# Two-layer network on one core: layer 1's expert places from running sums made batch by batch, with the expert stage begun earlier and its broadcasts spread out

## The chip, the cores and the metric

The kernel runs on one core of one Trainium2 chip. The number that counts is the device time of one execution in microseconds, as the median of several runs. Five engines work side by side, each through its own queue in order: TensorE (PE, with weight loads shown apart as PEld), VectorE (DVE), ScalarE (ACT), GpSimd (POOL) and SyncE (SP), which here only issues transfers.

## What is computed

Two layers over 16 sequences of 512 tokens with 128 features (8192 tokens). Layer 0 adds to its input a memory that is trained chunk by chunk and a transformer block with a dense mixture of 8 experts. Layer 1 adds causal attention (16 heads, a convolution, then a second attention pass over the same keys and values) and a routed mixture of 32 experts, of which each token chooses 8:

```python
x = L0_attn_x
xn = _layernorm(x, axis=-1)
x = x + _L0_attn_ref(xn, ...) + _L0_ffn_ref(xn, ...)
xn = _layernorm(x, axis=-1)
x = x + _L1_attn_ref(xn, ...) + _L1_ffn_ref(xn, ...)
```

The part that matters is the routing in `_L1_ffn_ref`. An expert takes at most 128 tokens, the first 128 in token order that chose it:

```python
probs = jax.nn.softmax(logits.astype(jnp.float32), axis=-1)
topw, topi = jax.lax.top_k(probs, TOP_K)
...
oh = jax.nn.one_hot(flat_e, E, dtype=jnp.int32)
pos = (jnp.cumsum(oh, axis=0) * oh).sum(-1) - 1
buf = jnp.zeros((E, CAPACITY, H), x.dtype).at[flat_e, pos].set(flat_x, mode='drop')
```

So for place c of expert e the kernel must find which token has it: the token at which the running count of choices of e reaches c + 1.

## The kernel before

**Turns.** All work is written as Python generators ("stages"). `Turns.run` steps every live stage once a turn, in the order of a small number given to each stage: 0 for `tops` (scores and their maxima, `largest`), 1 for `back` (scores again, exponentials, weighted values, `weighted`), 2 for `summed`, 3 for the expert stage `moe`, 4 for the projections and `middle`, 5 for `total`. PE's queue is exactly in this order, written out by hand. The queues of DVE, ACT, POOL and SP are put in order by the framework's scheduler, which goes by the program's order and by its own picture of when an instruction's inputs are ready. At the end of a turn with little PE work, `fill` adds a matmul of no use (L206).

Eleven turns make one unit of attention: for a quarter of a batch's work, row blocks of 512 (four turns), 384 (four), 256 (two) and 128 columns (one). In each turn two PSUM banks of scores go to DVE for the maxima (L396 for the wide ones, L403 and L404 for the narrow) and two to ACT for the exponentials (L476); POOL, and after the mark `counted` DVE (L482), clears what lies above the diagonal. Seven PSUM banks go round. `room` and `hold` limit how many of them the other stages may keep beyond a turn (`pools["work"]`: 3, then 2).

**Routing.** `middle(b)` ends layer 0 for batch b and routes it. It writes for each tile of 128 tokens the running counts by expert to the table `ctab` in DRAM (L1246) and each tile's totals into one column of `totT`, 32 experts by 64 tiles, in SBUF (L1247), eight transfers a batch on SP's queue; then it stores tokens and weights (`xw`, L1254) and marks `("xw", b)`.

**The expert stage.** `moe` starts when all batches are routed. Its first part sums `totT` along the tiles with six steps of two DVE instructions (L1349, L1350: shifts by 1, 2, 4, 8, 16, 32). `places(u)`, for eight experts at a time, multiplies the sums by a mask (`bd`, L1358), has PE broadcast them to 128 partitions (`pt`, two matmuls), counts on DVE how many tiles lie before each place (`le`, `istar`, L1366 and L1367) and takes the largest sum among them (`base`, L1369 and L1371). `side` starts the four `places` one turn apart. From these come the row indices `rowi` (L1376). POOL then gathers 32 rows of `ctab` (`gt`, L1387), DVE counts within each (`lt`, L1381), and the token indices follow. After that come 16 pairs of experts, one begun every third turn: POOL gathers the tokens (`xg`, L1425), PE and ACT compute, DVE weighs the result (`eo`, L1464), and POOL adds it to `acc` in DRAM by a scatter (L1470). Each scatter waits for the one before. When `moe` is marked, `total` copies the batches whose attention was added early straight to the output (L1497, thirteen of them) and adds up the others (L1500 to L1505).

**Around the change.** Layer 0's buffers `fa` are closed when its attention is done, and `fb` opens in their place; the exponentials then alternate between buffers in `att` and `mid`, later between `att` and `fb`. `lent` holds the exponentials in `mid` that are not used yet. The end of `network` reads, in the kernel before:

```python
turns.run(until=lambda: ("xw", B - 1) in done)
pools.update(weights=[att, fb])
turns.run(until=lambda: not lent)
...
pools["work"] = 2
turns.stages.append((turns.turn, 3, moe(mo)))
```

The second `run` waits until the last exponentials in `mid` have been read; only then is `mid` closed, `mo` opened in its place and `moe` begun. At the same time batch 15's projections for attention run (`front1`): `split_rows` writes `hi` (ACT, L333) and `lo` (DVE, L335), one buffer each, and stores each with two transfers (L339), first for the queries, two turns later for the keys.

Of the kernel before, what the change touches and what calls it, by code (L numbers as in the profile page):

```python
# [9 lines left out]
F32 = mybir.dt.float32  # L10
# [7 lines left out]
P = 128  # L18
# [64 lines left out]
def network(ctx: ExitStack, tc: tile.TileContext, a, out):  # L83
# [189 lines left out]
    def idle(n):  # L273
        for _ in range(n):
            yield
# [920 lines left out]
    def middle(mid, b):  # L1196

        yield from after(("ffn", b))
        ac = mid.tile([P, TB, D], F32, tag="am", bufs=2, name="am")
        nc.sync.dma_start(flat(ac), x1d[0, b])  # L1200
        xa = mid.tile([P, TB, D], F32, tag="st", bufs=4, name="xa")
        nc.sync.dma_start(xa, acc_b[b])
        x2 = mid.tile([P, TB, D], F32, tag="st", bufs=4, name="x2")
        yield from idle(2)
        yield from layernorm(x2, ac, row["g2"], row["b2n"])
        nc.gpsimd.tensor_tensor(x2, x2, xa, ALU.add)
        yield from idle(3)
# [12 lines left out]
        yield from room()  # L1220
        prl = work("prl")[:, 0 : TB * EXP1].rearrange("p (t e) -> p t e", e=EXP1)
        for t in range(TB):
            mm(prl[:, t, :], xT[:, t * P : (t + 1) * P], D1("gw"))
        lg = sm.tile([P, TB, EXP1], F32, tag="lg", name="lg")
        nc.scalar.copy(lg, prl)
        yield
        t8 = sm.tile([P, TB, TOPK], F32, tag="t8", name="t8")
        lr = sm.tile([P, TB, EXP1], F32, tag="lr", name="lr")
        for t in range(TB):
            nc.vector.max(t8[:, t, :], lg[:, t, :])  # L1230
            nc.vector.match_replace(lr[:, t, :], t8[:, t, :], lg[:, t, :], -BIG)
# [12 lines left out]
        for t in range(TB):  # L1244
            of = ct[EXP1 * t : EXP1 * (t + 1), :]
            nc.sync.dma_start(ctab_v[:, b * TB + t, :], of)  # L1246
            nc.sync.dma_start(totT[:, b * TB + t : b * TB + t + 1], of[:, P - 1 : P])  # L1247
        yield
        nc.vector.tensor_tensor(lg, lg, lr, ALU.mult)
        sw = sm.tile([P, TB], F32, tag="sw", name="sw")  # L1250
        nc.vector.tensor_reduce(sw, lg, AX.X, ALU.add)
        nc.vector.reciprocal(sw, sw)
        nc.vector.tensor_tensor(xwt[:, :, D:], lg, bc(sw, 2, EXP1), ALU.mult)
        nc.sync.dma_start(xw_b[b], xwt)  # L1254
        mark("xw", b)
        yield


# [79 lines left out]
    rowi = mw.tile([P, EXP1], I32, name="rowi")  # L1338
    tok = mw.tile([P, EXP1], F32, name="tok")

    def moe(mo):

        memE = load(mo, "mske", [EXP1, EXP1])

        cur = totT
        s_ = 1
        while s_ < NTILE:
            nxt = mo.tile([EXP1, NTILE], F32, tag=f"cum{s_}", bufs=1, name=f"cum{s_}")
            nc.vector.tensor_copy(nxt[:, 0:s_], cur[:, 0:s_])  # L1349
            nc.vector.tensor_tensor(nxt[:, s_:], cur[:, s_:], cur[:, : NTILE - s_], ALU.add)  # L1350
            cur, s_ = nxt, 2 * s_
        per = 512 // NTILE

        def places(u):

            es = slice(u * per, (u + 1) * per)
            bd = ff.tile([EXP1, per, NTILE], F32, tag="ew1", bufs=2, name="bd")
            nc.vector.tensor_tensor(bd, bc(cur, 1, per), bc(memE[:, es], 2, NTILE), ALU.mult)  # L1358
            yield
            yield from room()  # L1360
            pt = hold("pt")
            mm(pt, ones[0:EXP1, :], bd.rearrange("k e i -> k (e i)"))
            ptv = pt.rearrange("p (e i) -> p e i", i=NTILE)
            le = ff.tile([P, per, NTILE], F32, tag="ew2", bufs=2, name="le")
            yield
            nc.vector.tensor_scalar(le, ptv, col("iota"), None, ALU.is_le)  # L1366
            nc.vector.tensor_reduce(istar[:, es], le, AX.X, ALU.add)  # L1367
            yield
            nc.vector.tensor_tensor(le, le, ptv, ALU.mult)  # L1369
            drop()  # L1370
            nc.vector.tensor_reduce(base[:, es], le, AX.X, ALU.max)  # L1371
        yield from side(*[places(u) for u in range(EXP1 // per)])
        nc.vector.tensor_scalar(base, base, -1.0, col("iota"), ALU.mult, ALU.add)
        rowf = mo.tile([P, EXP1], F32, tag="rowf", bufs=1, name="rowf")
        nc.vector.scalar_tensor_tensor(rowf, istar, float(NTILE - 1), C1("eoff"), ALU.min, ALU.add)
        nc.vector.tensor_copy(rowi, rowf)  # L1376
        gts = []

        def count(e):
            lt = mo.tile([P, P], F32, tag="lt", name="lt")  # L1380
            nc.vector.tensor_scalar(  # L1381
                lt, gts[e], base[:, e : e + 1], None, ALU.is_le, ALU.add, accum_out=tok[:, e : e + 1]
            )

        for e in range(EXP1):
            gt = mo.tile([P, P], F32, tag="gt", bufs=12, name="gt")
            nc.gpsimd.indirect_dma_start(  # L1387
                out=gt, out_offset=None, in_=ctab,
                in_offset=bass.IndirectOffsetOnAxis(ap=rowi[:, e : e + 1], axis=0),
                bounds_check=EXP1 * NTILE - 1, oob_is_err=True,  # L1390
            )
            gts.append(gt)
            if e >= 8:
                count(e - 8)
            if e % 3 != 0:
                yield
# [6 lines left out]
        gidf = mo.tile([P, EXP1], F32, tag="gidf", bufs=1, name="gidf")  # L1403
        nc.vector.tensor_scalar(gidf, tok, float(N - 1), None, ALU.min)
        gidx = mo.tile([P, EXP1], I32, tag="gidx", bufs=1, name="gidx")
        nc.vector.tensor_copy(gidx, gidf)

        inv = mo.tile([P, EXP1], F32, tag="inv", bufs=1, name="inv")
        nc.vector.tensor_scalar(inv, tok, float(N), col("iota"), ALU.is_ge, ALU.mult)
        nc.vector.scalar_tensor_tensor(inv, tok, float(N), inv, ALU.min, ALU.add)  # L1410
        sidx = mo.tile([P, EXP1], I32, tag="sidx", bufs=1, name="sidx")
        nc.vector.tensor_copy(sidx, inv)
        yield

        def fetch(e2):
            es = slice(2 * e2, 2 * e2 + 2)
# [237 lines left out]
```

## Time and profile before

| | us |
|---|---|
| median of 3 runs | 3565.93 (3565.69 to 3568.84) |
| the profiled execution, its own time | 3557.66 |
| its span, first to last instruction | 3555.9 |
| PE busy in the span | 3379.7 (95%) |
| DVE busy | 2315.6 (65%) |
| ACT busy | 2233.4 (63%) |
| POOL busy | 1508.2 (42%) |
| last totals of batch 15 issued (L1247) | 3260.98 |
| running sums begin (L1349) | 3265.17 |
| first broadcast begins (`pt`) | 3269.08 |
| first gather of `ctab` (L1387) | 3300.43 |
| first and last scatter (L1470) | 3378.07, 3526.19 |

The mean granted clock of TensorE is 0.975 of full speed. Times within the execution are counted from the span's start. A wait is shown in brackets behind the instruction that ended it, with what released it; a wait for several things is put down to the one that came last. Busy PE time includes the matmuls of `fill` and takes no account of the clock.

### The profile page before, as it was taken

The numbers are of one execution on the slowest core, as the hardware profiler recorded it, in microseconds if no ns is written. First come the engines' busy times: TensorE is split into PE (matmuls) and PEld (weight loads), VectorE is DVE, ScalarE is ACT, GpSimd is POOL, SyncE is SP. The second block draws the span as 40 slices with busy tenths as digits, with TensorE's granted clock in tenths as the row PEclk, the third lists the DMA queues.
The fourth block names the chain that finished last, engine by engine and source line by source line (L and its number), as shares of the span: only waits on it lengthen the run. The fifth ranks groups of instructions, "written<-read, shape, count | busy, mean of one in ns | idle before, by whom it ended". The sixth has DMA issues, their size and how long they took to land.

```text
span 3555.9 us, 63951 instructions
## 1 busy us (share of the span) xinstructions
PE 3379.7 (95%) x22085; PEld 1897.3 (53%) x22085; DVE 2315.6 (65%) x6045; ACT 2233.4 (63%) x4951; POOL 1508.2 (42%) x2354
## 2 busy tenths in 40 slices
PE   6999999999999999999999999999999999998887
PEld 3445555554555555455555565555555555554443
DVE  5676666656766566556467667666666666567875
ACT  1566766775766787666656666665666666664444
POOL 5323432432431455432544344443444344433654
PEclk7999999999999999999999999999999999998998
DMA  5222222222122332443434443444344443433343
GB/s 178 70 71 77 71 82 74 74 77 83 56 85 86 102 109 87 133 122 102 135 108 122 124 125 115 130 126 121 107 122 122 124 125 98 134 106 98 93 102 93
DMA packets 289794, 370.37 MB, mean 104 GB/s; under 512 B 45984, under 2 KB 141376, under 8 KB 289088
## 3 DMA queue, kind: packets, MB, share of 16 engines
q1 hardware_dynamic: 282304, 359.46, 35.0%
q0 software_dynamic: 7168, 6.82, 1.2%
q8 instruction: 177, 2.90, 0.3%
q14 instruction: 145, 1.19, 0.1%
HBM read 236.58 MB, written 132.99 MB: 104 GB/s over the span
## 4 chain that ended last, share of the span: by engine, by line
PE 50%; DVE 5%; DMA 3%; ACT 1%; POOL 1%; issue 1%; SPq 1%; POOLq 0%; DVEq 0%; ACTq 0%
PE s L197 13%; PE pye L611 10%; PE phe L197 10%; PE pc L197 9%; PE pq L197 1%; DVE s L396 1%; PE fill L206 1%; DVE nm L404 1%; PE tpc L252 1%; PE tp L252 1%; DVE s L403 1%; PE po L197 1%; ACT e L476 1%; DMA rq<-lo 1%; PE pv L197 1%
## 5 line engine op out<-in xcount | busy, mean ns | idle before, releaser
L476 ACT ACTIVATE e<-s 128x512 f32<-128x512 f32 (+1 forms) x2432 | 1278.3, 577 | 556.4 <-PE s L197 517.2
L404 DVE TENSOR_REDUCE nm<-s 128x1 f32<-128x512 f32 (+2 forms) x1408 | 907.5, 682 | 510.1 <-PE s L197 509.2
L396 DVE CUSTOM_DVE_ANT_0 s<-s,sb_const 128x512 f32<-128x512 f32 (+1 forms) x1024 | 623.4, 643 | 390.3 <-PE s L197 388.9
L484 POOL TENSOR_SCALAR_AFFINE_SELECT e<-e 128x128 f32<-128x128 f32 (+2 forms) x1270 | 429.6, 347 | 751.0 <-ACT e L476 726.5
L197 PE MATMUL s<-kx,qx 64*128 64x512 f32 (+3 forms) x3072 | 620.4, 429 | 26.8 <-DMA kx<-rk 13.5
L197 PE MATMUL pc<-e,vp 128*32 128x512 f32 (+3 forms) x6144 | 621.7, 502 | 13.9 <-POOL e L484 7.8
L611 PEld LDWEIGHTS pye<-ew,hTe 128*128 128x128 f32 x4096 | 519.0, 192 | 178.7 <-issue 157.9
L197 PEld LDWEIGHTS s<-kx,qx 64*128 64x128 f32 x3072 | 271.2, 187 | 555.2 <-issue 219.4
L611 PE MATMUL pye<-ew,hTe 128*128 128x128 f32 x4096 | 562.3, 281 | 1.5 <-ACT hTe L601 1.4
L197 PE MATMUL s<-qx,kx 64*128 64x512 f32 (+3 forms) x3072 | 535.7, 356 | 27.2 <-DVE nm L404 8.4
L197 PE MATMUL phe<-x1T,ew 128*128 128x512 f32 x1024 | 551.1, 623 | 7.8 <-DMA ew<-in_ew 3.1
L601 ACT ACTIVATE hTe<-phe,sb_cols 128x512 f32<-128x512 f32 x512 | 354.1, 692 | 245.2 <-PE phe L197 242.8
L197 PEld LDWEIGHTS s<-qx,kx 64*128 64x128 f32 x3072 | 305.5, 188 | 80.4 <-ACT e L476 19.1
L619 POOL TENSOR_TENSOR ac<-ac,y 128x512 f32<-128x512 f32 x128 | 163.9, 1280 | 425.9 <-ACT y L618 363.9
L403 DVE TENSOR_TENSOR s<-s,sb_const 128x256 f32<-128x256 f32 (+1 forms) x384 | 181.6, 515 | 190.5 <-PE s L197 157.4
L197 PEld LDWEIGHTS pc<-e,vp 128*32 128x32 f32 x6144 | 151.4, 110 | 238.1 <-issue 173.2
L197 PEld LDWEIGHTS phe<-x1T,ew 128*128 128x128 f32 x1024 | 158.8, 193 | 75.0 <-issue 44.1
L618 ACT ACTIVATE y<-pye,pr 128x128 f32<-128x128 f32 x512 | 147.5, 370 | 30.6 <-PE pye L611 26.2
L396 DVE DVE_READ_ACCUMULATOR2_ANT nm<- 128x1 f32 x1024 | 144.1, 141 | 0.0
L213 POOL TENSOR_SCALAR rs_t<-ss 128x4 f32<-128x4 f32 (+1 forms) x56 | 12.0, 215 | 221.5 <-ACT sq L266 220.0
L1470 POOL DMA_INDIRECT acc<-eo,sidx x32 | 52.0, 1624 | 72.2 <-DVE eo L1464 26.3
L213 POOL TENSOR_SCALAR rs_t<-ln_mv 128x4 f32<-128x4 f32 x64 | 12.8, 200 | 162.3 <-DVE ln_mv L223 159.4
(302 smaller groups left out, 3906.4 us busy)
## 6 DMA issues: line engine op xcount, KB each, us to landing
ew<-in_ew SPq DMA_DIRECT2D x256, 256.0 KB
kx<-rk SPq DMA_DIRECT2D x192, 256.0 KB
qx<-rq SPq DMA_DIRECT2D x128, 256.0 KB
rq<-hi SPq DMA_DIRECT2D x64, 256.0 KB
rq<-lo SPq DMA_DIRECT2D x64, 256.0 KB
rk<-hi SPq DMA_DIRECT2D x64, 256.0 KB
rk<-lo SPq DMA_DIRECT2D x64, 256.0 KB
qx<-r SPq DMA_DIRECT2D x64, 256.0 KB
```

The costliest lines, as they stand in the source:

```text
L197: nc.tensor.matmul(o, lhsT=lhsT, rhs=rhs, start=start, stop=stop)
L252: nc.tensor.transpose(tp[:, t * P : (t + 1) * P], src(t), ident)
L396: newest[0] = nc.vector.tensor_tensor_reduce(out=sv[r][:, 0, :], in0=sv[r][:, 0, :], in1=row["caus"][:, S - n :], scale=1.0, scalar=-BIG, ...
L403: nc.vector.tensor_tensor(dg, dg, bc(row["caus"][:, S - P :], 1, per), ALU.add)
L404: newest[0] = nc.vector.tensor_reduce(nm[:, qt, r, t : t + per], sv[r], AX.X, ALU.max)
L476: nc.scalar.activation(e[:, r, 0 : per * n], s[r], AF.Exp, scale=SCALE)
L484: cleared[0] = nc.gpsimd.affine_select(out=ev[:, r, :, 0:P], in_=ev[:, r, :, 0:P], pattern=[[0, per], [1, P]], compare_op=ALU.is_ge, fill= ...
L601: nc.scalar.activation(hs[i], ph, AF.Relu, bias=col("fb", i))
L611: nc.tensor.matmul(pye[0][:, t, :], lhsT=h[:, t * P : (t + 1) * P], rhs=w2[e][:, f, :], start=(f == 0 and t == 0), stop=(f == 3), skip_gro ...
L618: nc.scalar.mul(y[:, t, :], pye[0][:, t, :], pr[:, t, e : e + 1])
L619: nc.gpsimd.tensor_tensor(ac, ac, y, ALU.add)
L1470: nc.gpsimd.indirect_dma_start(out=acc, out_offset=bass.IndirectOffsetOnAxis(ap=sidx[:, e : e + 1], axis=0), in_=eo[:, i, :], in_offset=No ...
```

## The change

Four things are done to the start of layer 1's expert stage.

- The running sums of the totals are made in `middle`, batch by batch: three idle turns after `xw`, four small DVE instructions add up the four columns of the batch and the last sum of the batch before, into a new tile `upto`. The twelve instructions of the sums over all 64 columns go.
- `moe` is begun as soon as batch 15's `xw` is marked, without the wait for `lent`, but waits for the mark `("upto", B - 1)`. Its small tiles move from `mo` to `fb` (the gathers' buffers from twelve to ten), and the stage takes `mo` only when it comes to the pairs. The mask is loaded with layer 1's other constants.
- The broadcast of each `places` comes two turns after its product instead of one.
- The four `places` begin two turns apart instead of one.

```diff
+        yield from idle(3)
+        of = totT[:, b * TB : (b + 1) * TB]
+        ups = sm.tile([EXP1, TB], F32, tag="ups", name="ups")
+        nc.vector.tensor_copy(ups[:, 0:1], of[:, 0:1])
+        nc.vector.tensor_tensor(ups[:, 1:], of[:, 1:], of[:, : TB - 1], ALU.add)
+        to = upto[:, b * TB : (b + 1) * TB]
+        carry = upto[:, b * TB - 1 : b * TB] if b else 0.0
+        nc.vector.tensor_scalar(to[:, 0:2], ups[:, 0:2], carry, None, ALU.add)
+        nc.vector.scalar_tensor_tensor(to[:, 2:], ups[:, 2:], carry, ups[:, 0:2], ALU.add, ALU.add)
+        mark("upto", b)
         yield
...
-    def moe(mo):
-
-        memE = load(mo, "mske", [EXP1, EXP1])
-
-        cur = totT
-        s_ = 1
-        while s_ < NTILE:
-            nxt = mo.tile([EXP1, NTILE], F32, tag=f"cum{s_}", bufs=1, name=f"cum{s_}")
-            nc.vector.tensor_copy(nxt[:, 0:s_], cur[:, 0:s_])
-            nc.vector.tensor_tensor(nxt[:, s_:], cur[:, s_:], cur[:, : NTILE - s_], ALU.add)
-            cur, s_ = nxt, 2 * s_
+    upto = mw.tile([EXP1, NTILE], F32, name="upto")
+    memE = load(mw, "mske", [EXP1, EXP1])
+
+    def moe():
+
+        yield from after(("upto", B - 1))
...
-            nc.vector.tensor_tensor(bd, bc(cur, 1, per), bc(memE[:, es], 2, NTILE), ALU.mult)
-            yield
+            nc.vector.tensor_tensor(bd, bc(upto, 1, per), bc(memE[:, es], 2, NTILE), ALU.mult)
+            yield from idle(2)
...
-        yield from side(*[places(u) for u in range(EXP1 // per)])
+        yield from timed(*[(2 * u, places(u)) for u in range(EXP1 // per)])
...
-            gt = mo.tile([P, P], F32, tag="gt", bufs=12, name="gt")
+            gt = fb.tile([P, P], F32, tag="gt", bufs=10, name="gt")
...
+        while "mo" not in pools:
+            yield
+        mo = pools["mo"]
...
-        pools.update(weights=[att, fb])
+        pools.update(weights=[att, fb], work=2)
+        turns.stages.append((turns.turn, 3, moe()))
         turns.run(until=lambda: not lent)
     with tc.tile_pool(name="mo", bufs=2) as mo:
-        pools["work"] = 2
-        turns.stages.append((turns.turn, 3, moe(mo)))
+        pools["mo"] = mo
```

`timed`, which layer 0 uses already, starts each part at the turn given with it:

```python
def timed(*parts):
    parts, at = list(parts), 0
    while parts:
        parts = [(t, g) for t, g in parts if t > at or next(g, StopIteration) is not StopIteration]
        at += 1
        yield
```

More of the change, by code (lines that the diff above doesn't have):

```diff
@@ L1371, in places @@
             nc.vector.tensor_reduce(base[:, es], le, AX.X, ALU.max)
-        yield from side(*[places(u) for u in range(EXP1 // per)])
+        yield from timed(*[(2 * u, places(u)) for u in range(EXP1 // per)])
         nc.vector.tensor_scalar(base, base, -1.0, col("iota"), ALU.mult, ALU.add)
-        rowf = mo.tile([P, EXP1], F32, tag="rowf", bufs=1, name="rowf")
+        rowf = fb.tile([P, EXP1], F32, tag="rowf", bufs=1, name="rowf")
         nc.vector.scalar_tensor_tensor(rowf, istar, float(NTILE - 1), C1("eoff"), ALU.min, ALU.add)
@@ L1379, in count @@
         def count(e):
-            lt = mo.tile([P, P], F32, tag="lt", name="lt")
+            lt = fb.tile([P, P], F32, tag="lt", bufs=2, name="lt")
             nc.vector.tensor_scalar(
@@ L1402, in moe @@
         nc.vector.scalar_tensor_tensor(tok, istar, float(P), tok, ALU.mult, ALU.add)
-        gidf = mo.tile([P, EXP1], F32, tag="gidf", bufs=1, name="gidf")
+        gidf = fb.tile([P, EXP1], F32, tag="gidf", bufs=1, name="gidf")
         nc.vector.tensor_scalar(gidf, tok, float(N - 1), None, ALU.min)
-        gidx = mo.tile([P, EXP1], I32, tag="gidx", bufs=1, name="gidx")
+        gidx = fb.tile([P, EXP1], I32, tag="gidx", bufs=1, name="gidx")
         nc.vector.tensor_copy(gidx, gidf)
-        inv = mo.tile([P, EXP1], F32, tag="inv", bufs=1, name="inv")
+        inv = fb.tile([P, EXP1], F32, tag="inv", bufs=1, name="inv")
         nc.vector.tensor_scalar(inv, tok, float(N), col("iota"), ALU.is_ge, ALU.mult)
         nc.vector.scalar_tensor_tensor(inv, tok, float(N), inv, ALU.min, ALU.add)
-        sidx = mo.tile([P, EXP1], I32, tag="sidx", bufs=1, name="sidx")
+        sidx = fb.tile([P, EXP1], I32, tag="sidx", bufs=1, name="sidx")
         nc.vector.tensor_copy(sidx, inv)
         yield
+        while "mo" not in pools:
+            yield
+        mo = pools["mo"]
         def fetch(e2):
```

## The prediction

> **What bounds the kernel now.** I began at the end of the program, with the chain of waits (start, duration, what), because PE's 95% busy share is an average in which filler matmuls count too.
>
> ```profile
> 3526.19 3.42 DMA acc<-eo,sidx
> ...
> 3539.85 5.11 DMA fin<-ao
> ...
> 3546.38 2.84 DMA fin<-ao
> 3549.33 1.29 POOLq L1650
> ```
>
> The chain does not end in attention. It ends in layer 1's expert work: the last scatter-add lands at 3529.6, then SP issues thirteen copies to the output, then the last two sums are loaded, added and stored. The span ends 26.3 us after that landing. The last attention matmul ends at 3545.4, and what follows it is finished before the chain's last store lands. So the kernel ends when the scatters end, plus 26 us. Next, the timeline of POOL, which issues them:
>
> ```profile
> 3518.15 1.55 POOL L1470 DMA_INDIRECT acc<-eo,sidx  x1 [2.43 <-DVE e L482]
> 3522.04 1.77 POOL L1470 DMA_INDIRECT acc<-eo,sidx  x1 [2.34 <-DVE e L482]
> 3526.19 1.65 POOL L1470 DMA_INDIRECT acc<-eo,sidx  x1 [2.39 <-DVE rec L510]
> ```
>
> Each scatter starts some 4.1 us after the last: 1.6 us of POOL, then 2.4 us whatever engine is named, which is the landing of the scatter before. The 16 pairs take 3378 to 3526, 9.3 us a pair. Before that, POOL runs the 32 gathers of L1387 without a real gap: 44.17 us busy of the 52.11 between 3299.46 and 3351.57 (last row of the second fence below), the rest being 0.17 to 0.3 us of issue at each. So from the moment when the row indices exist (`rowi`, L1376, ready at 3299.46) the expert chain runs at POOL's own pace to the end. **What matters is when rowi is ready.** The stretch before it, in the timeline of all engines:
>
> ```profile
> 3265.17 0.14 DVE L1349 COPY cum<-totT 32x1 f32<-32x1 f32 x1 [2.56 <-DMA totT<-ct]
> 3267.68 0.75 DVE L335 SCALAR_TENSOR_TENSOR lo<-pjk,sb_cols,hi 128x512 fp32r<-128x512 f32 x1 [0.69 <-DMA rq<-lo]
> 3268.35 1.27 DVE L1358 TENSOR_TENSOR bd<-cum,sb_mske 32x512 f32<-32x512 f32 x2
> 3269.08 2.07 PE L197 MATMUL pt<-bd,sb_const 32*128 32x512 f32 x2 [6.24 <-DVE bd L1358]
> 3271.80 0.57 DVE L396 CUSTOM_DVE_ANT_0 s<-s,sb_const 128x384 f32<-128x384 f32 x1 [2.17 <-PE s L197]
> ```
>
> PE, in its fixed order, stands 6.24 us at the first broadcast. DVE was late for two reasons: it waited for the last totals to land (3265.17), and then for a store out of `lo`, which has one buffer (3267.68). Busy time by stretch (PE, PEld, DVE, ACT, POOL, then PE's granted clock):
>
> ```profile
> 3240.00:3244.00 4.00, 4.00 (x29) 2.27 (x30) 1.95 (x4) 2.21 (x4) 0.78 (x3) 0.50 0.47 156
> 3268.00:3272.00 4.00, 2.92 (x6) 1.00 (x6) 1.82 (x4) 0.00 (x0) 0.00 (x0) 0.50 0.85 287
> 3284.00:3288.00 4.00, 4.00 (x14) 1.22 (x18) 2.12 (x6) 0.87 (x2) 0.45 (x3) 0.50 0.01 2
> 3288.00:3292.00 4.00, 3.73 (x19) 0.92 (x11) 3.41 (x11) 0.50 (x2) 0.27 (x1) 0.88 0.00 0
> 3268.35:3299.46 31.11, 26.63 (x121) 11.42 (x121) 26.39 (x62) 9.94 (x20) 6.65 (x19) 0.67 0.38 103
> 3299.46:3351.57 52.11, 44.38 (x284) 19.88 (x280) 39.37 (x145) 22.07 (x44) 44.17 (x69) 0.97 0.43 108
> ```
>
> After the pause PE ran at half clock until about 3289. But look at DVE between 3268.35 and 3299.46: 26.39 us busy of 31.11. PE's pause is the striking thing; DVE's queue is what rowi waits for.
>
> **The change in turns.** Call T the turn in which batch 15's `xw` is marked. From PE's order in the timeline T+3 starts at 3261.00, T+4 at 3271.08 (after the first broadcast) and T+11 at 3294.02. Before: the first product `bd` is in T+2, the broadcasts in T+3, T+4, T+7, T+8 (`room` holds the last two back), rowi in T+11. After: `xw`, three idle turns, so `upto` is marked in T+3; the expert stage stands ahead of it in a turn and sees it in T+4. Products in T+4, 6, 8, 10, broadcasts in T+6, 8, 10, 12, last maximum in T+14, rowi in T+15. "Without a pause" takes away one turn of waiting for lent buffers; the idle turns give back more: the experts start two turns later and their indices come **four turns later**, counted in turns.
>
> **The cost of each part.** (1) Removed: twelve DVE instructions of the cum chain, 3265.17 to 3267.0, 1.8 us. They lie in a wait: `lo` could not start before 3267.68 in any case. Gain 0. (2) Moved: PE no longer stands 6.24 us, since T+4 and T+5 have no broadcast. In its place PE comes to T+5 at about 3265 and finds the score banks of T+4 unread, because DVE stands at `totT` (3265.17) and `lo` (3267.68): I expect a pause of 0 to 2.5 us there. (3) Broadcasts: 1.04 us each at full clock, where a filler of 1.06 us would stand; 0. (4) DVE up to rowi. Before, 26.39 us of work after `lo` (ends 3268.35). It now has four more turns' maxima to do ahead of rowi, all 384 wide: two instructions of 0.51 us to the next start, 1.03 a turn, 4.1 us. That makes 30.5 us. Against it, w: maxima of T+4 (1.03) and T+5 (two adds, two reductions, 1.86) that DVE does while it would wait, 0 to 2.9 us; I take 1.9, since the order between them and `lo` is not to be seen. And i: DVE idle, 0 (broadcasts spread out) to 4.72 (as before: 31.11 − 26.39); I take 1.0, as PE's clock should suffer less. rowi = 3268.35 + 30.5 − 1.9 + 1.0 = 3297.95, **1.5 us earlier**; at the ends 3295.95 (−3.5) and 3303.6 (+4.1). (5) Ten instead of twelve gather buffers: gather e would wait for count e−10; the closest is gather 14 at 3323.18, count 4 ended 3318.80: 4.4 us of room, 0. (6) SP: the load of the 32x32 mask leaves 3265.17 (0.44 us) for the start of layer 1, where nothing waits for it; expert weights are still loaded once `mo` is open, some 80 us before use. `work=2` one turn earlier holds no one: the projections hold one bank at a time. (7) Sixteen times four small DVE instructions, 0.14 to 0.20 us by the cum rows, 0.7 us a batch, with a wait for the totals. Batch 7, the timelines of SP and DVE:
>
> ```profile
> 2325.70 0.51 SPq L1247 DMA_DIRECT2D totT<-ct  x1
> ...
> 2328.54 0.57 DVE L396 CUSTOM_DVE_ANT_0 s<-s,sb_const 128x384 f32<-128x384 f32 x1 [2.29 <-PE s L197]
> ...
> 2331.36 0.57 DVE L396 CUSTOM_DVE_ANT_0 s<-s,sb_const 128x384 f32<-128x384 f32 x1 [1.68 <-PE s L197]
> ```
>
> The last issue ends at 2326.21. In batch 15 the totals landed 3.6 us after the issue (3261.54 to 3265.17); the quickest small transfer in view, `qx<-top`, 1.7 us (3236.17 to PE's start at 3237.85). So they land at 2327.9 to 2329.8. Three turns on, the new work stands after the maxima of 2328.54 to 2329.67, in a gap of 1.68 us: cost 0. What queues behind it on DVE is the next turn's maxima, and PE's score banks wait for those (in batch 15 also `lo` and the first `bd`). If DVE's queue has it at 2326.2 instead, the maxima come up to 2.0 us late; DVE's waits for `rq<-lo` (4.5 us, four times) passed 1.8 us on to PE, so 0.4 of it, 0.8 us a batch, 12 us in all. I take 0. A part of the 12 counts in a rival.
>
> **Two rules against the rows.** The Trainium skill, "TensorE: Matmul & The Clock Gate", section "What's actually happening", has the clock halved after an idle window of about 3.4 us and restored after a busy one as long. This case disagrees both ways: 2.0 us without a matmul (3235.85 to 3237.85) left the clock at 0.50 in 3240 to 3244, and after 6.24 us it stayed there for 20 us with PE 66 to 100% busy. By the rule, part (2)'s pause costs no clock, i is 0, and the estimate is 3563 (3563.4); by the rows, 3564 (3564.4). The Trainium skill's "DMA: Bandwidth & Descriptors", section "Anatomy of one DMA — SWDGE (gpsimd) path", puts the fixed cost of a transfer that GpSimd issues at about 2.0 us; by that estimate part (7) is free wherever it is queued, while the 3.6 us of batch 15 leave the 12 us open.
>
> **The sum.** The profiled execution took 3557.66 (span 3555.9), 8.3 below the median of the runs, 3565.93; a shift of rowi moves both alike. 3565.93 − 1.5 = **3564**, which is no change that can be told: 0.2%, 7.1 us, is about what a measurement of this kernel resolves. Its own bounds are 3562 to 3570.
>
> **Rivals.** *PE sets the pace after all* (faster). If DVE gets ahead of its queue, the turns go at PE's undisturbed pace: seven turns from 3246.22 to 3261.00, 2.11 each. T+15 then starts at 3261 + 12 × 2.11 = 3286.3, and rowi follows 2 to 5.4 us later (before: 3299.46 − 3294.02): 8 to 11 earlier, **3556**. For it: the 6.24 us and twenty slow microseconds are real, and attention will be four turns ahead. Against it: DVE's 30.5 us of work. *The clock stays down* (slower, one mechanism: T+5, a PE pause of about 2 us, as at 3235.85). Then the twelve turns go on at T+4 to T+11's own pace, (3294.02 − 3271.08) / 7 = 3.28 each. T+15 is T+4 (3262.8 to 3269) plus 36.1, rowi 5.4 later: 3304 to 3310, 5 to 11 late, **3574**. It decides once the half clock lasts about as long as now. *The totals stop DVE in every batch* (slower): 12 us, **3578**, from 1.2 us of late maxima a batch on (15 × 0.4 × 1.2 = 7.1). *The earlier start does nothing*, as buffers keep the work in its old place: 3566, inside the forecast.
>
> **Chances.** Forecast 0.42; PE's pace 0.31; clock 0.18; totals 0.07; nothing done 0.02. So faster 0.31, same 0.44, slower 0.25. The range reaches from a little below the faster rival's 3556 to just short of 3578: 3554 to 3577.
>
> **What would show it.** Right: rowi within 4 us of 3299.5 although attention is then four turns further; the gathers still some 51 us; the last scatter to the end still 26 us; DVE over 85% busy before rowi. Part (2): PE's longest pause near 3265 at most 2.5 us. Part (7): no DVE wait for `totT` over 0.5 us in batches 0 to 14. Wrong: a rowi at 3292 or below, a clock at 0.50 from 3268 to beyond 3285, such DVE waits with PE's banks behind them, or pairs that go quicker than 9.3 us now that attention is ahead.

## The result, and the profile after

The changed kernel is slower: 3576.35 us (median of 10 runs, 3571.06 to 3588.98) against 3565.81 for the kernel before beside it (10 runs), a ratio of **1.0033, 95% interval 1.0021 to 1.0045**: 11.7 us. A second measurement, on another chip, gave 1.0020 (1.0011 to 1.0029), 7.1 us. The forecast was 3564, no change that can be told; the time lies inside its range (3554 to 3577), but its account of the cause did not hold.

Single executions of one kernel differ by several us either way, so what a change is worth is taken from the ratios, and what the profiles show is compared from a mark close by: the copy of batch 15's running counts, `ct` (L1243). I profiled both kernels twice. In us after `ct`:

| | before | before, again | after | after, again |
|---|---|---|---|---|
| `rowi` | 43.99 | 43.69 | 48.35 | 48.71 |
| first scatter | 122.76 | 123.25 | 131.44 | 131.76 |
| last scatter | 270.88 | 273.20 | 286.66 | 284.18 |
| attention's last matmul (`po`) | 289.67 | 290.88 | 291.25 | 288.17 |
| end of the span | 300.65 | 304.07 | 317.38 | 314.01 |
| `ct` itself | 3255.30 | 3261.44 | 3255.16 | 3263.14 |

All of the loss lies behind `ct`. Over all profiles of this document `ct` itself stands at 3260.4 us on average, in the thirteen with the small steps and in the seven without (single ones from 3254 to 3267), so the fifteen batches ahead of it cost nothing that shows. In the means of the two profiles each, the changed kernel is some 4.7 us late at `rowi`, 4 more by the first scatter, 4 to 5 more by the last, and next to none in the end behind it: 13.3 us, somewhat more than the ratios give. Attention is not later at all. The end of the chain of waits in the changed kernel (start, duration, what) has the form that it had before:

```profile
3541.82 3.28 DMA acc<-eo,sidx
...
3562.91 2.91 DMA fin<-ao
```

From the last scatter's landing (3545.10) to the end are 27.4 us, where 26.3 had been. So the kernel still ends with its scatters; they come later. First, `rowi`. Busy time by stretch, with the columns of the prediction's second fence:

```profile
3268.35:3303.52 35.17, 23.63 (x145) 9.51 (x145) 27.06 (x69) 11.32 (x23) 8.72 (x23) 0.81 0.48 130
3303.52:3355.39 51.87, 45.34 (x281) 19.52 (x280) 40.03 (x151) 22.45 (x47) 44.00 (x71) 1.00 0.38 97
```

From the same place, DVE did 27.06 us of work in 35.17: it stood 8.11 us. The gathers in the second row take their 51.87 us as before. Where DVE stood, and why, is in the changed kernel's timeline:

```profile
3264.42 0.39 SPq L1335 DMA_DIRECT2D xs<-acc  x1
3264.90 0.93 SPq L339 DMA_DIRECT2D rq<-hi  x2
...
3270.32 0.73 DVE L335 SCALAR_TENSOR_TENSOR lo<-pjk,sb_cols,hi 128x512 fp32r<-128x512 f32 x1
...
3275.05 0.33 SPq L373 DMA_DIRECT2D kx<-rk  x1
...
3278.33 0.76 PE L197 MATMUL s<-kx,qx 64*128 64x512 f32 x1 [7.33 <-DMA kx<-rk]
3279.13 0.70 DVE L396 CUSTOM_DVE_ANT_0 s<-s,sb_const 128x512 f32<-128x512 f32 x1 [3.02 <-PE s L197]
...
3282.51 0.70 DVE L396 CUSTOM_DVE_ANT_0 s<-s,sb_const 128x512 f32<-128x512 f32 x1 [2.62 <-PE s L197]
...
3287.43 0.70 DVE L396 CUSTOM_DVE_ANT_0 s<-s,sb_const 128x512 f32<-128x512 f32 x1 [2.44 <-PE s L197]
```

PE's pause of 6.24 us at the first broadcast is gone, and a pause of 7.33 us stands nine microseconds further on, for the key rows of batch 15's first attention unit. They land at a time of their own, whatever PE has done by then, so what PE gained before it waited away here. And they land later than before: SP now has a load ahead of the stores of the query rows, `xs<-acc` (the sum that `last` makes for batch 12), for which it stood until 3264.42. `lo` has one buffer and waits for those stores (before: 3267.68, now 3270.32), the key rows' stores wait for `lo`, and `kx` is issued 19.9 us after `ct` instead of 17.2.

Second, the way from `rowi` to the last scatter. The prediction read POOL's waits as landings of the scatter before. Here is POOL's group of scatters from the first to the last, before and after (count, busy, mean ns, idle time ahead of them and its releasers; the second row leaves out the last scatter):

```profile
L1470 POOL DMA_INDIRECT acc<-eo,sidx x32 | 52.0, 1624 | 72.2 <-DVE eo L1464 26.3 <-DMA acc<-eo,sidx 18.7 <-DVE e L482 8.4
```

```profile
L1479 POOL DMA_INDIRECT acc<-eo,sidx x31 | 50.0, 1612 | 79.3 <-DVE eo L1473 31.4 <-DVE e L482 27.9 <-DMA acc<-eo,sidx 14.1
```

The rows need care. Of the 72.2 us before, 13.3 lie ahead of the first scatter (in the share of `eo`), and of the 79.3 us after, 14.5 (in the share of `e`); and the engine named is not always what a scatter waited for, as the prediction said. So I count a wait as one for the product `eo` where the scatter starts less than 1 us behind the product's end. Behind the first scatter these waits make 16.3 and 16.6 us in the two profiles of the kernel before, and 28.8 and 22.9 us in the two of the changed kernel. Only from the last such wait on do the scatters go one behind the other, 4.1 to 4.6 us apart on average: the last five before, the last eleven and fifteen in the changed kernel. The prediction had shown the last three, and read them rightly; it took them for all 32. And the chain of waits of the kernel before, in this stretch, which I had not looked at (some of its longest pieces):

```profile
3370.96 1.85 PE pc L197 x16
...
3400.15 3.57 PE pc L197 x16
...
3420.78 1.75 POOL xg L1425
...
3431.66 6.42 DMA acc<-eo,sidx
...
3472.41 3.57 PE pc L197 x16
3475.98 1.44 PE pgu L197 x8
```

From the first scatter to the last, 43% of it is PE, 25% DVE, 14% transfers and 7% POOL: much of it attention's products (`pc`), with the experts' (`pgu`) among them. POOL waits there for PE, which comes to a pair when its fixed order comes to it. The first pair shows it best. These are its transposes on PE, before and after:

```profile
3364.17 0.44 PE L1436 MATMUL tpx<-sb_const,xg 128*128 128x128 f32 x2
```

```profile
3374.45 0.44 PE L1445 MATMUL tpx<-sb_const,xg 128*128 128x128 f32 x2
```

That is 108.87 and 119.29 us after `ct`, 10.4 us later for four turns. Neither shows a wait: POOL was done with the gathers of the pair's rows at 103.92 and 111.56, and the rows lay ready when PE came.

### The profile page after: what moved, and what is told of

It is laid out like the page before. It is cut to its first block, busy times and chain, and to the rows that moved or that the text cites. A ratio compares the mean times of both kernels' runs of the same rounds, so it can differ in the third digit from the quotient of the medians.

```text
span 3572.5 us, 64003 instructions
## 1 busy us (share of the span) xinstructions
PE 3381.2 (95%) x22081; PEld 1899.5 (53%) x22081; DVE 2320.7 (65%) x6087; ACT 2230.4 (62%) x4951; POOL 1506.0 (42%) x2364
## 4 chain that ended last, share of the span: by engine, by line
PE 50%; DVE 3%; DMA 3%; POOL 2%; issue 1%; ACT 1%; SPq 1%; POOLq 0%; DVEq 0%; ACTq 0%
PE s L197 13%; PE pye L611 10%; PE phe L197 10%; PE pc L197 9%; PE pq L197 1%; PE tpc L252 1%; DVE s L396 1%; PE fill L206 1%; PE tp L252 1%; DVE nm L404 1%; PE po L197 1%; PE pjk L197 1%; DVE s L403 0%; PE pv L197 0%; POOL gt L1392 0%
## 5 line engine op out<-in xcount | busy, mean ns | idle before, releaser
L213 POOL TENSOR_SCALAR rs_t<-ln_mv 128x4 f32<-128x4 f32 x64 | 12.7, 198 | 162.4 <-DVE ln_mv L223 159.5
```

## The experiments

The theories at the start: *turns* (each turn by which the indices come later against attention costs some 3 us), *key rows* (PE's new pause), *small steps* (the sixteen sums cost DVE time); later *POOL's own pace*, the prediction's rule, against *the pairs' place in PE's order*. In what follows T is the turn in which batch 15's `xw` is marked; turns are counted by the kernel's own `turn`. Three slips in the expectations: `xs<-acc` is batch 12's, not batch 13's; `room` holds the broadcasts back, so that rowi is in T+14 in e1, e4 and e5; and the turn that they give for the last scatter is that of the last pair's first scatter, one turn earlier, as in the table. The times after `ct` come from one profiled execution each, the ratios from all; the profiled execution was 9.3 us above the median of its run in e1, 12.3 in e11 and 12.7 in e17.

| run | rowi after `ct` | first pair | last pair's first scatter | ratio to before, interval |
|---|---|---|---|---|
| before (e0: again) | 44.0 (43.7) | T+39 | T+91 | 0.9999 (0.9986 to 1.0012) |
| after; e16: again | 48.4; 48.7 | T+43 | T+95 | 1.0033; 1.0020 (1.0011 to 1.0029) |
| e1 sums alone | 52.1 | T+42 | T+92 | 1.0003 (0.9992 to 1.0015) |
| e3 spacing alone | 49.0 | T+41 | T+91 | 1.0000 (0.9988 to 1.0011) |
| e4 after, old spacing | 51.7 | T+42 | T+92 | 1.0010 (0.9997 to 1.0022) |
| e5 before, all 4 turns later | 49.2 | T+42 | T+92 | 1.0029 (1.0015 to 1.0043) |
| e6, e18 sums at once | 45.8, 45.8 | T+40 | T+90 | 0.9990 (0.9978 to 1.0003), 0.9999 (0.9987 to 1.0011) |
| e7 after, 17 turns of gathers | 48.4 | T+39 | T+90 | 1.0012 (1.0003 to 1.0022) |
| e8 before, 16 turns of gathers | 43.8 | T+34 | T+85 | 1.0021 (1.0012 to 1.0030) |
| e9 after, pairs 2.5 turns apart | 48.5 | T+42 | T+86 | 1.0024 (1.0013 to 1.0035) |
| e10 before, pairs 2.5 turns apart | 45.3 | T+38 | T+80 | 1.0072 (1.0059 to 1.0085) |
| e11 after, `xs` late | 47.7 | T+43 | T+95 | 1.0013 (1.0005 to 1.0022) |
| e12 both of e7 and e11 | 48.0 | T+39 | T+90 | 1.0002 (0.9993 to 1.0012) |
| e13 e6, 20 turns of gathers | 45.5 | T+39 | T+90 | 1.0000 (0.9991 to 1.0009) |
| e14 e6, `xs` late | 41.9 | T+40 | T+90 | 0.9996 (0.9983 to 1.0009) |
| e15 after, unit later | 53.1 | T+43 | T+95 | 1.0020 (1.0008 to 1.0032) |
| e17 before, pairs 4 turns later | 47.3 | T+43 | T+93 | 1.0035 (1.0021 to 1.0049) |

### The parts alone (e1, e3, e4, e5)

e1 takes from the change only the `upto` steps:

```diff
-        cur = totT
...
+        yield from after(("upto", B - 1))
...
-            nc.vector.tensor_tensor(bd, bc(cur, 1, per), bc(memE[:, es], 2, NTILE), ALU.mult)
+            nc.vector.tensor_tensor(bd, bc(upto, 1, per), bc(memE[:, es], 2, NTILE), ALU.mult)
```

e3 takes only the spacing into the kernel before; e4 takes the spacing out of the changed kernel:

```diff
-            yield
+            yield from idle(2)
...
-        yield from side(*[places(u) for u in range(EXP1 // per)])
+        yield from timed(*[(2 * u, places(u)) for u in range(EXP1 // per)])
```

e5 is the kernel before with `yield from idle(4)` at the head of `moe`.

> The running sums made batch by batch, and nothing else of the change: the expert stage begins where it did, with its own buffers (twelve for the gathers) and the old spacing of the broadcasts. The row indices (rowi) come in turn T+13 instead of T+11. Theory A, turns: each turn by which rowi comes later against attention costs what the whole change cost per turn, 11.7 / 4 = 2.9 us, so this is 5.9 us slower than before. Theory B, key rows: the load xs<-acc of batch 13 now stands in SP's queue ahead of the stores of batch 15's query rows, as in the changed kernel (and not as before, where it came some 30 us later); the key rows of batch 15's first unit land 2.5 us later, PE stands over 6 us for them, and this is 8 to 12 us slower. Theory C, the sixteen small steps cost DVE in every batch: 5 to 12 us slower, and visible at batch 12 already.

> Only the spacing of the broadcasts: two turns behind their products and two turns apart, in the kernel before. The row indices come in turn T+13, as in the run with the sums alone. Theory A, turns: 5.9 us slower. Theory B, key rows: xs<-acc of batch 13 stands in SP's queue behind the stores of batch 15's query and key rows, so PE's wait for the key rows is shorter than 5 us, and the time is within 3 us of before. Theory C, the small steps: none here, so no change.

> The changed kernel with the old spacing: a broadcast one turn behind its product, products in successive turns. The row indices come in turn T+13 instead of T+15. Theory A, turns: 5.9 us slower than before. Theory B, key rows: xs<-acc of batch 13 stands ahead of the query rows' stores as in the changed kernel: 8 to 12 us slower. Against the run with the sums alone this differs by ten gather buffers instead of twelve, by their place and by work=2 a turn earlier: if these cost nothing the two are within 3 us of each other.

> The kernel before with four idle turns put in front of the expert stage's first instruction, nothing else: rowi comes in turn T+15 as in the changed kernel, with the old chain of sums, the old spacing and the old buffers. Theory A, turns: 11.7 us slower, like the changed kernel. Theory B, key rows: xs<-acc of batch 13 stands ahead of the query rows' stores here too, so 8 to 12 us slower. Theory C, the small steps in every batch: none here, so 0 to 4 us slower only. PE's pause at the first broadcast should be gone (under 1 us), and its longest pause should be the one for kx<-rk.

No part alone costs what the whole does: 1.1, 0.0 and 3.6 us. The small steps cost nothing that shows, and e4 against e1 shows nothing for ten buffers and their place. e5, which has none of the change but its delay, is 10.3 us slower. Theory B does not hold as the main cause: e4 has PE's pause for the key rows (6.10 us) and rowi 7.7 us late, and loses 3.6 us; e1, with the load ahead of the query rows and rowi 8 us late, loses at most 5.3 us by its interval (PE's long pause is there still at the first broadcast, 6.25 us, and not at the key rows). e3 has rowi 5.0 us late, its last pair in the old turn, and loses nothing. A flat price per turn does not fit either: e1, e4 and e5 have first and last pair in the same turns, the last one turn later than before, and 1.1, 3.6 and 10.3 us. I have not found what makes e5 the slowest of them; in its profile PE is idle for 51.6 us from `ct` to attention's last matmul, against 46.1 and 43.5 in e1's and e4's.

### The pairs' place in PE's order (e7 to e10, e17)

e7 and e8 change only how often the loop over the gathers lets a turn pass; e9 and e10 change `at % 3 == 2` to `at % 5 in (1, 3)`; e17 puts `yield from idle(4)` ahead of the first gather of rows. e7:

```diff
-            if e % 3 != 0:
+            if e % 3 != 0 and e > 5:
                 yield
```

> The changed kernel, with four turns fewer given to the 32 gathers (no turn between the first six), so that the row indices still come in turn T+15 but the first pair starts in turn T+39, as in the kernel before, and the last scatter's turn is one earlier than before (T+90, against T+91 before and T+95 in the changed kernel). Theory of the prediction (POOL's own pace from the row indices to the end): nothing is gained, 3575 to 3579, 11 us slower than before. Theory A, turns: a turn of the pairs lasts about 3 us (before: 47 turns from the first scatter to the last in 148 us), the last scatter's turn decides, so 3 us faster to equal: 3562 to 3567. Between the two, if POOL cannot issue the gathers in 17 turns: 3568 to 3573.

> The kernel before with 16 turns instead of 21 for the 32 gathers, nothing else: the last scatter's turn is T+85 instead of T+91. POOL's own pace: the gathers stand back to back already (44 of 52 us busy), so no change, 3564 to 3568. Theory A, turns: six turns of 3 us, 18 us faster, 3548, less what POOL's pace takes back. Theory D, PE waits in its order for gathered rows that are not there: first tpx with a pause of over 5 us on PE, and 3570 to 3580.

> The changed kernel with a pair every two and a half turns instead of every three: the last scatter in turn T+86 instead of T+95. POOL's own pace: 9.3 us a pair as before, no change from the changed kernel, 3575 to 3579. Theory A, turns: nine turns of 3 us, 27 us faster than the changed kernel where nothing else stops it; two scatters of 4.1 us a pair are a floor, 16 x 8.2 = 131 us against the 155 us that the pairs took in the changed kernel, so 3550 to 3560.

> The kernel before with a pair every two and a half turns: the last scatter in turn T+80 instead of T+91. POOL's own pace: no change, 3564 to 3568. Theory A, turns, with the floor of 4.1 us a scatter: the pairs take 131 to 140 us instead of 148, 8 to 17 us faster, 3549 to 3558. Where the scatters then come back to back, the idle time before them names the landing of the scatter before, about 2.4 us each.

> The kernel before with four idle turns between the row numbers (gidx) and the first gather of rows, nothing else: rowi keeps its turn and its time, the first pair stands in T+43 as in the changed kernel instead of T+39. This prices the pairs' place alone. If the two parts are right (about half of the loss from the pairs' place, half from late row indices), 4 to 7 us slower than before. If the expert chain goes at POOL's own pace from the row indices on, POOL stands four turns of 2.4 to 3.3 us, and the end comes 10 to 13 us later. If the place costs nothing and only rowi counts, POOL catches up: within 2 us of before.

e7 leaves rowi where the change put it and gives the pairs their old turns: 4.3 us over before instead of 7.1 to 11.7. e17 leaves rowi in its turn and moves the pairs alone: 12.5 us, as much as the whole change (3.4 us of its profile's delay are chance, at rowi). That is more than the 4 to 7 expected, and what "POOL stands four turns" would give; but POOL does not stand there. The first rows are gathered 4.4 us behind the last gather of counts, as before (4.3), and then POOL waits 21.35 us for the first product (before: 13.33), since PE comes to the first pair only 126.62 us after `ct`. It waits for products, not for its own work, from the first scatter on:

```profile
L1470 POOL DMA_INDIRECT acc<-eo,sidx x31 | 49.9, 1610 | 86.7 <-DVE eo L1464 44.4 <-DMA acc<-eo,sidx 11.2 <-DVE e L482 10.1
```

A place ahead of its data is no better. e8, e9 and e10, for which the turns theory expected gains of 6 us and more, are 7.5, 8.6 and 25.7 us slower than before. For e8 a pause of over 5 us was expected at the first pair's transposes; there is none, and the longest, 5.63 us, is at the tenth pair's. In e10 PE reaches pairs whose rows are not there. The group of the pairs' transposes in the kernel before and in e10 (idle time and releasers behind the second bar):

```profile
L1436 PE MATMUL tpx<-sb_const,xg 128*128 128x128 f32 x32 | 8.2, 314 | 12.6 <-DMA xg<-xw,gidx 11.6 <-DVE nm L396 0.7 <-DVE eo L1464 0.3
```

```profile
L1436 PE MATMUL tpx<-sb_const,xg 128*128 128x128 f32 x32 | 9.2, 334 | 23.7 <-DMA xg<-xw,gidx 23.7
```

In e8 and e10 attention, which stands behind the pairs in PE's order, becomes the end: its last matmul comes 24.8 and 43.1 us later than before. e10's chain of waits:

```profile
3535.36 3.23 DMA acc<-eo,sidx
...
3588.22 1.51 PE po L197 x8
```

The waits for rows are only a part of this: from `ct` to attention's last matmul PE is idle for 73.3 us in e10, against 45.4 before, and e7, e12 and e13 wait 19 us at these transposes without such a loss. That the pairs stand too early in e8 to e10 is what the runs suggest; why it costs so much is not shown.

It looks like a trough, with edges that overlap. With three turns to a pair, the kernels whose first pair stands in T+39 to T+41 lie between 0.9990 and 1.0012; T+42 and T+43 are at 1.0003 to 1.0035, and T+34 at 1.0021. By the last pair it is as clear: T+90 and T+91 at 0.9990 to 1.0012, T+92 at 1.0003 to 1.0029, T+93 and T+95 at 1.0013 to 1.0035.

### The key rows (e11, e12, e15)

e11 moves one load, `xs<-acc` of batch 12, behind the key rows; every other instruction keeps its turn. e12 has this and e7's loop. e15 begins two units of batch 15 later (`12 + 8 * c` for `16 + 8 * c` in `begun`).

```diff
+            if b == B - 4:
+                yield from idle(8)
             x2 = l1.tile([P, TB, D], F32, tag="st", bufs=2, name="xs")
```

> The changed kernel with one load moved: xs<-acc of the last batch that takes it (batch 12) eight turns later, behind the loads of batch 15's key rows on SP, as the kernel before had it; every other instruction keeps its turn. Theory B, key rows: they land 2.6 us earlier (kx is issued 17.2 us after the counts ct instead of 19.9), PE's pause for them falls from 7.3 to 4.7 us, rowi comes 2 to 3 us earlier (45.5 to 46.5 us after ct), and the time falls by as much, to 8 to 10 us over before. If DVE's queue or the turns set rowi, the pause shrinks and rowi stays at 48.4: no change from the changed kernel, 11.7 us over before.

> The changed kernel with both: xs<-acc eight turns later, and the gathers in 17 turns instead of 21, so that the first pair stands in turn T+39 as before. If the slowdown is the sum of the two (about 4.3 us for rowi, of which the key rows make 2.6, and 7.4 us for pairs four turns later), this is 1 to 2 us over before, 3 us below the run with 17 turns alone. If they are not independent: as that run, 4.3 us over before.

> The changed kernel with the first two attention units of batch 15 begun four turns later, so that PE has other work in the turns in which it stood for their key rows. If PE's pause for kx<-rk is what made rowi late: the pause falls below 3 us, DVE's idle time before rowi from 8.1 to under 5 us, and rowi comes 43 to 46 us after ct instead of 48.4. If DVE's own queue sets rowi: 47 us or more. The end may well be later, as attention ends about four turns later.

In e11 `kx` is issued 18.7 us after `ct`, only 1.2 us earlier, PE's pause is 6.15 instead of 7.33, and rowi comes 0.6 earlier, not 2.6. Its time, 4.6 us over before, is better than that explains; against the changed kernel's two measurements the gain is 2.5 to 7.1 us, and it may be partly chance. e12 is within 0.2% of before (0.7 us), though its rowi is 4 us late. e15 missed its aim: the unit waits for the rows' mark, PE's pause was there as before (7.54 us), and nothing follows from it for the question.

### The sums at once (e6, e13, e14, e18), and the two kernels again (e0, e16)

e6 takes `yield from idle(3)` out ahead of the sums, and rowi comes in T+12. e13 gives the gathers one turn less as well; e14 has e11's load besides; e18 repeats e6.

> The kernel before once more, for a second profile of it: ratio 1.000 within 0.2%. From batch 15's counts (ct) to rowi the first profile had 44.0 us, and from rowi to the end of the span 256.7 us; both within 3 us here if the first profile is typical. If rowi comes 48 us or more after ct, the later rowi of the changed kernel (48.4) is no loss at all.

> The changed kernel without the three idle turns in front of the running sums: rowi in turn T+12, the first pair in T+40 (before: T+39, changed kernel T+43), and xs<-acc of the last unfinished batch stands behind the stores of the query rows on SP. DVE now meets the totals before they land in every batch. Theory A2 (four turns in the pairs' start cost 7 us, rowi's delay 4): first pair one turn later than before, so 2 us, and rowi as before, so 0 to 2 us: 0 to 4 us slower than before. The prediction's rival of stops in every batch: 7 to 12 us slower, with DVE waits of 1 us or more for totT in batches 0 to 14. POOL's own pace from rowi on: the time follows rowi alone.

> The run with the sums at once (rowi in T+12), with one turn fewer for the gathers, so that all pairs stand in the turns of the kernel before (first in T+39) or earlier. If the later turn of the pairs still cost something in that run, this one is 1 to 3 us faster than it, 4 to 7 us faster than before. If row indices 2 us later than before now meet pairs that are due, PE waits for gathered rows and it is the same as before or slower.

> The run with the sums at once, and xs<-acc of batch 12 eight turns later, behind the loads of the key rows. If the load's place on SP is worth what it seemed in the changed kernel (7 us in the medians, though rowi came only 0.6 us earlier), 3 to 7 us faster than the run without it. If that gain was mostly the scatter of single executions, or is bound up with the 7.3 us pause that this kernel does not have, within 2 us of it.

> The changed kernel once more on the chip of these runs: ratio 1.002 to 1.0045 again, rowi 48.3 to 48.5 us after ct, and a second measure of the pairs, which took 155.2 us in the first profile (before: 148.1 and 149.9). If they take 152 us or less here, the 7 us in the first profile were partly chance.

> The run with the sums at once, once more, as the version that might beat both kernels: it gave 0.9990 with an interval from 0.9978 to 1.0003. If the gain is real, again 0.998 to 0.9995; if it was chance, 0.9995 to 1.001. Either way 7 us or more below the changed kernel.

e13, expected 1 to 3 us faster than e6, is not. In e16 the pairs take 152.4 us from the first scatter to the last, so some of the first profile's 155.2 was chance. e14 shows the key rows' part cleanly. PE has no pause for `kx` (e6: 2.42 us), and DVE's idle time ahead of rowi, in its group of attention's maxima, falls by half. e6, then e14:

```profile
L396 DVE CUSTOM_DVE_ANT_0 s<-s,sb_const 128x512 f32<-128x512 f32 (+1 forms) x13 | 8.2, 646 | 6.2 <-PE s L197 6.2
```

```profile
L396 DVE CUSTOM_DVE_ANT_0 s<-s,sb_const 128x512 f32<-128x512 f32 (+1 forms) x13 | 8.2, 647 | 3.3 <-PE s L197 3.3
```

rowi comes 3.8 us earlier, all else in the same turns. And it is worth nothing that shows: 0.9996 against 0.9990 and 0.9999. Where it went stands in the timelines of POOL and PE, at the last gather of rows ahead of the first scatter and at the first pair's transposes. e6, then e14:

```profile
3371.93 1.01 POOL L1433 DMA_INDIRECT xg<-xw,gidx  x1 [0.30 <-issue]
...
3372.42 0.33 PE L1444 MATMUL tpx<-sb_const,xg 128*128 128x128 f32 x1
...
3387.62 1.68 POOL L1478 DMA_INDIRECT acc<-eo,sidx  x1 [14.68 <-DVE eo L1472]
```

```profile
3368.68 1.01 POOL L1435 DMA_INDIRECT xg<-xw,gidx  x1 [0.30 <-issue]
...
3374.45 0.69 PE L1446 MATMUL tpx<-sb_const,xg 128*128 128x128 f32 x2
...
3390.10 1.69 POOL L1480 DMA_INDIRECT acc<-eo,sidx  x1 [20.41 <-DVE eo L1474]
```

The rows are gathered 5.2 us earlier after `ct`, but PE comes to the pair 111.36 and 111.39 us after it, at the same time, and POOL waits 20.41 us instead of 14.68. e6 seemed to beat the kernel before; e18 does not confirm it. Both are equal to it and 7 us or more better than the changed kernel.

## Why the prediction was wrong

**The step that failed** is this one: "the expert chain runs at POOL's own pace to the end", and with it "What matters is when rowi is ready". rowi 3.8 us earlier gave nothing that shows (e14 against e6), rowi 4 to 5 us later cost 0.0 to 4.3 us with the last pair in its old turn or a turn earlier (e3, e12, e7), and the pairs moved with rowi in its turn cost 12.5 us (e17). The prediction's own rows held the sign: 31 steps of 4.1 us are 127 us, and its scatters took 148. Between the first gather of rows and the last scatter the pairs stand at fixed places among attention's matmuls, and PE comes to them in its own time. The prediction had the number that mattered, "four turns later", and converted it into time at rowi alone. PE's time to a given place hardly changed (attention's last matmul 291.3 and 288.2 us after `ct`, before 289.7 and 290.9; PE idle from `ct` to that matmul 45.6 and 46.1 us, before 45.4 and 44.6, the profile's gaps added up), so what was put four turns further on in its order ended later: the last scatter now comes 4 us ahead of attention's last matmul, where it came 18 ahead, and attention covers 4 of the 30 us behind it instead of 18.

**How the loss divides.** e7 and e12 put the pairs back and leave 4.3 and 0.7 us; by the ratios, then, 0.7 to 4.3 of the 7.1 to 11.7 come from the late row indices, and the rest from the pairs' place. The division is no finer than that, and the clock blurs it. Among executions of the kernel before, those with a lower mean granted clock are longer: by 2.1 us for each 0.001 in the 35 beside e12 (correlation −0.79), by 2.6 in the 23 beside e17 (−0.83). e17 ran at 0.9694 on average and before beside it at 0.9718, e12 at 0.9736 and before at 0.9716. Set to one clock by the slope among the executions of the kernel before beside each run, which is an estimate, e17 loses 6.8 us instead of 12.5, e7 and e12 lose 4.7 and 5.3 instead of 4.3 and 0.7, e16 loses 7.4 instead of 7.1, and e14 lies 2 to 3 us below e6 and e18. The pairs' place costs something either way; that rowi is worth nothing is not safe. Whether the edits move the clock or chance did is not shown.

**Part (4)**, rowi: w, DVE's work done ahead, was 30.5 − 27.06 = 3.4 us (bound 2.9, taken 1.9), and i, DVE's idle time, 8.1 (bound 4.72, taken 1.0). 3268.35 + 30.5 − 3.4 + 8.1 = 3303.5, 4.1 us late, with DVE 77% busy where over 85% had been named: "DVE's queue is what rowi waits for" was so before, and no longer after the change. **Part (2)** looked at the right place only: near 3265 there is no pause, but the longest one, 7.33 us, stands at 3278. **Part (6)** named the mask's load, and not the load `xs<-acc` that moves ahead of the query rows, on which part (2)'s pause hangs in part (e11, with the load back behind the key rows: 6.15 us).

**Right** were part (3), a broadcast's two matmuls take 1.09 to 1.12 us in all; (5), the gathers' 51 us with ten buffers (51.87); (7), no wait of DVE for `totT` in the changed kernel, and with the sums at once one of 1.66 us in batch 15 (e6) and none over 0.3 us ahead of it (e6, e13, e14, e18), so the third rival is out; and the 26 us behind the last scatter's landing (27.4). That the removed chain lay in a wait, part (1), no run tests by itself.

**The rivals.** *PE's pace* had its mechanism: with the first broadcast in T+6, PE was 11.7 us ahead of before at the last scores ahead of the key rows (15.37 us after `ct` against 27.04), and 4.0 behind its two pauses there (26.55 against 30.53). *The clock stays down* named a time near the right one (3574) with a mechanism that is not there: from PE's restart at 3278.33 the clock was back by 3285, seven turns before rowi; and the changed kernel's executions had no lower clock than before's beside them (e16: 0.9716 and 0.9709 on average).

## What to carry to other kernels

On an engine with one fixed order, a stage that is put later in that order comes later by the work that is put ahead of it, even if its data are early (the first pair, 10.4 us for four turns); read its place there before its data's time. Follow the chain of waits through the whole stage, not only at its end: in the profile of before it named PE and DVE for 68% of the pairs' time, and POOL for 7%. And when a pause is taken away, ask which input lands next at a time of its own; that one takes the pause over.

## What was not expected of the hardware

How long the half clock lasts after a pause is not the same from one execution to the next. In the two profiles of the kernel before and in those of e8, e10 and e17, which are the same up to there, PE restarts at the first broadcast after 6.24, 6.07, 6.21, 6.42 and 6.58 us. In the first the clock is back at 3289, 20 us later; in the second, in e8 and in e10 it takes 19.7, 19.6 and 21.5 us. The second (restart at 3275.03) and e17 (restart at 3278.61), by stretch, the granted clock in the third column from the end:

```profile
3287.44:3291.44 4.00, 2.63 (x4) 0.78 (x3) 3.30 (x6) 1.19 (x2) 0.58 (x2) 0.50 0.01 2
3291.44:3295.44 4.00, 4.00 (x21) 1.09 (x20) 2.82 (x10) 0.87 (x2) 0.58 (x2) 0.59 0.00 0
```

```profile
3294.49:3298.49 4.00, 4.00 (x18) 1.09 (x20) 2.29 (x8) 0.87 (x2) 0.59 (x2) 0.50 0.00 0
...
3310.49:3314.49 4.00, 4.00 (x20) 1.41 (x22) 2.91 (x9) 1.08 (x2) 1.59 (x3) 0.50 0.26 74
```

In e17 it takes 36.5 us, with PE busy in whole stretches of 4 us, and its rowi is 3.4 us later for nothing else that I can see. After the changed kernel's 7.33 us PE stood once more, 2.61 us, and had the full clock some 3 us after it went on for good (3281.71; the clock is 0.50 in 3282.16 to 3284.16 and 0.83 in 3284.16 to 3286.16). The Trainium skill, "TensorE: Matmul & The Clock Gate", section "What's actually happening", restores the clock after a busy window of about 3.4 us. The changed kernel's two profiles agree (3.8 us in the second); the other five do not. A few us of any single profile of this stage are such chance.
